# Two more quads of edges bucketed in the last round of a graph-convolution kernel

## Chip, core and metric

The kernel runs on one core of a Trainium2 chip. The metric is the device time of one execution in microseconds (us). The program is one launch; all times below are of that one core.

## What is computed

A pre-normalised graph convolution over 6250 nodes with 128 features and 200000 edges. Cut to what matters:

```python
h = maximum(layernorm(x), 0)
xw = h @ W_in                                       # per node
W_ij = (softplus(f_ij @ W_f1 + b_f1) - log 2) @ W_f2 + b_f2
m = xw[idx_j] * (W_ij * cutoff)                     # per edge; idx_j = dst
out = segment_sum(m, idx_i, num_segments=6250)      # idx_i = src
result = x + (softplus(out @ W_o1 + b_o1) - log 2) @ W_o2 + b_o2
```

`dst` is sorted, `src` is random. So the gather by `dst` reads narrow windows of a table, while the sum by `src` has to spread every edge's row over all nodes.

## The kernel before

**Tiling.** The edges are padded to 200704 (704 filler edges, with weight 0 and `src` 0) and worked in 391 *quads* of 512 edges, four chunks of 128 each. The main loop (its body is written out by the program) has one iteration i per quad, and a software pipeline runs through it: iteration i does the first matmul and the softplus of quad i, the gather matmuls and the second matmul of quad i-1 (`s2_pe_x`, `s2_pe_w`, L336 to L347), the scaling on ScalarE (L352), and the product m on VectorE (L357).

**Two ways to sum by node.** A *plain* quad is summed within each chunk by a matmul with an equality matrix (`s1_eq` L318, `s3_pe` L369), copied out of PSUM (`s3_copy` L377, five buffers `s`), given its row numbers (`s3_idx` L391, `s3_ji` L398), and added to an accumulator in DRAM by GpSimd: `scatter`, L417, one indirect DMA with add for each chunk. Four accumulators take turns (`acc_of`); one of them, accumulator 0, takes no scatter from number `RET` on, the total less 64, so that it can be read back into the SBUF accumulator `accT` during the last iterations (`r0_load` L866, `r0_tp` L873, `r0_add` L880).

A *bucketed* quad sends nothing by itself. Its 512 edges are ranked into 16 buckets of 392 nodes with 32 slots each, with 64 overflow slots for what finds no room (`rank_group` to `rank_slot`, one call for each eight quads). `perm_oh` (L503) builds a permutation matrix, `part_rem` (L517, L520) splits the messages into three bf16 parts, `permute` (L527, four matmul groups s = 0 to 3) sorts them into the slots, and `perm_out` (L533) copies each group to a tile `mst`. The overflow of two bucketed quads together goes through a short chain (`over_pe` L542 to L544, `over_out`, `over_idx`, `over_dg`, `over_row` L571, `over_eq` L576, `over_sum` L581, `over_copy`, `over_ji`, `over_int`) to a single scatter.

**Rounds and units.** Eight bucketed quads make a round. A round's slots are added up in SBUF by four *units*, one for each s: `unit_oh` (L605) builds a one-hot tile for each quad on VectorE, `unit_pe` (L620) runs 12 matmuls for each quad into four PSUM banks of tag B, all four of them, and `unit_evac` (L631) adds the four banks to `accT`. A unit's matmuls are in iteration k, its `unit_oh` in k-1, its `unit_evac` in k+1.

**Which quads, and where.** `sorted_quads` starts at quad 8 and steps by 2 and 3 in turn while q < 391 - `MPEND`, then cuts the list to full rounds: with `MPEND` 4 it is 8, 10, 13, ... 383, 385, that is 152 quads, 19 rounds. `unit_slots` puts the units of a round into iterations of the next round; those of the last round come at its last quad + 6, + 8, + 10, + 12: 391, 393, 395, 397. All of this is an order written out by hand: the hooks `at(i, point, ...)` fix each engine's program order, and each engine works in that order.

**After the loop** a flag is computed from the largest overflow (`dmax`, L994, to `flagi`, L1004). If a quad's overflow has exceeded its 64 slots, a loop over all 1563 chunks (L1007) does the sum again in a slow way; otherwise the loop runs no trip. Then the tail loads accumulators 1 to 3 (`t_load`, L1075), adds them (L1081, L1087), adds `accT` (L1098) and applies the output layers.

Of the kernel before, what the change touches and what calls it, by code (L numbers as in the profile page):

```python
# [7 lines left out]
F32 = mybir.dt.float32  # L8
BF16 = mybir.dt.bfloat16
# [11 lines left out]
P = 128  # L21
# [5 lines left out]
SLOTS = GRP * CAP + OVC  # L27
MP0 = 8
MPGAPS = (2, 3)
MPEND = 4  # L30
RND = 8
RKQ = 8
PW = 387
MW = 388
# [12 lines left out]
def tile_gnn(ctx: ExitStack, tc: tile.TileContext, x, fB, cT, srcT, srcr, dstr, win_, wf1, wf2, bias, bo1c, wo1,  # L47
# [20 lines left out]
    GN = NP // GRP  # L68
# [4 lines left out]
    mpq = sorted_quads(NQ)  # L73
# [12 lines left out]
    cp = ctx.enter_context(tc.tile_pool(name="cp", bufs=1))  # L86
# [3 lines left out]
    wk = edge.enter_context(tc.tile_pool(name="wk", bufs=2))  # L90
# [19 lines left out]
    win_sb = cp.tile([P, P], F32, name="win_sb")  # L110
    w1f = wk.tile([K1, P], F32, tag="a", name="w1f")
    w2 = cp.tile([P, P], F32, name="w2")
    bf = cp.tile([P, P], F32, name="bf")
    bo2b = cp.tile([P, P], F32, name="bo2b")
    bo1_sb = cp.tile([P, 1], F32, name="bo1_sb")
    nbo1 = cp.tile([P, 1], F32, name="nbo1")
# [10 lines left out]
    thr = cp.tile([P, GRP - 1], F32, name="thr")  # L127
    ge = cp.tile([P, 4 * RKQ, GRP + 1], BF16, name="ge")
    dropT = cp.tile([P, EP // P], BF16, name="dropT")
# [44 lines left out]
    def prep_norm(g):  # L174
        o, T = groups[g]
        rs = wk.tile([P, 4], F32, tag="rs", name="rs", bufs=1)
        r0 = pst[g]["r0"]
        nc.vector.tensor_tensor(rs[:, :T], r0[:, :T], r0[:, :T], op=ALU.mult)
        nc.vector.tensor_tensor(rs[:, :T], rs[:, :T], pst[g]["var"][:, :T], op=ALU.mult)
        nc.vector.tensor_scalar(rs[:, :T], rs[:, :T], -0.5, 1.5, op0=ALU.mult, op1=ALU.add)  # L180
        nc.vector.tensor_tensor(rs[:, :T], rs[:, :T], r0[:, :T], op=ALU.mult)
        xn = wk.tile([P, 4, P], F32, tag="rm", name="xn", bufs=1)
        for t in range(T):
            nc.vector.tensor_scalar(xn[:, t], x_sb[:, o // P + t], pst[g]["mv"][:, t, 0:1], rs[:, t:t + 1],
                                    op0=ALU.subtract, op1=ALU.mult)
        pst[g]["xn"] = xn
# [7 lines left out]

    def prep_relu(g):
        T = groups[g][1]
        h = wk.tile([P, 4, P], F32, tag="h", name="h", bufs=1)
        nc.scalar.activation(h[:, :T], pst[g]["hps"][:, :T], AF.Relu)
        pst[g]["h"] = h

# [6 lines left out]

    def prep_x1(g):
        T = groups[g][1]
        x3 = wk.tile([P, 4, 3, P], BF16, tag="x3", name="x3", bufs=1)  # L210
        nc.scalar.copy(x3[:, :T, 0], pst[g]["xs"][:, :T])
        pst[g]["x3"] = x3

    def prep_rm(g):
        T = groups[g][1]
        rm = wk.tile([P, 4, P], F32, tag="rm", name="rm", bufs=1)
        nc.vector.tensor_tensor(rm[:, :T], pst[g]["xs"][:, :T], pst[g]["x3"][:, :T, 0], op=ALU.subtract)
        pst[g]["rm"] = rm

# [201 lines left out]
    mp = {}  # L421
# [5 lines left out]
    def rank_group(r):  # L427
        qs = mpq[RKQ * r:RKQ * r + RKQ]
        nc4 = 4 * len(qs)
        srcf = wk.tile([P, 4 * RKQ], F32, tag="srcf", name="srcf", bufs=1)  # L430
        for k, q, d, n in runs(qs):
# [5 lines left out]
                                thr.unsqueeze(1).to_broadcast(n), op=ALU.is_ge)  # L437
        G = wk.tile([P, 4 * RKQ, GRP], BF16, tag="G", name="G", bufs=1)
        nc.vector.tensor_tensor(G[:, :nc4], ge[:, :nc4, :GRP], ge[:, :nc4, 1:], op=ALU.subtract)
        cnt = wk.tile([P, 4 * RKQ], F32, tag="cnt", name="cnt", bufs=1)  # L440
        nc.vector.tensor_reduce(cnt[:, :nc4], ge[:, :nc4, 1:GRP], axis=AX.X, op=ALU.add)
        loc = wk.tile([P, 4 * RKQ], F32, tag="loc", name="loc", bufs=1)
        nc.vector.scalar_tensor_tensor(loc[:, :nc4], cnt[:, :nc4], float(-GN), srcf, op0=ALU.mult, op1=ALU.add)
# [85 lines left out]
        mp[q]["q", s] = t  # L529

    def perm_out(q, s):
        mp[q]["ms", s] = wk.tile([P, MW], BF16, tag=f"ms{s}", name="mst", bufs=RND + 2 * s)
        nc.scalar.copy(mp[q]["ms", s][:, :PW], mp[q].pop(("q", s))[:, :PW])  # L533

    def over_pe(q):
# [63 lines left out]
        scatter(mp[q]["os"][:, :P], mp[q]["ji"][:, 0:1])  # L599

    def unit_oh(r, s):
        for q in mpq[r * RND:(r + 1) * RND]:
            so = wk.tile([P, GN], BF16, tag="so", name="so", bufs=RND)
            w = mp[q]["ms", s].bitcast(F32)
            nc.vector.tensor_scalar(so, iotw[:, :GN], w[:, 3 * P // 2:3 * P // 2 + 1], None, op0=ALU.is_equal)  # L605
            mp[q]["oh"] = so
# [3 lines left out]
    def unit_pe(r, s):  # L610
        ts = []
        for g in range(4):
            t = ps.tile([P, 512], F32, tag="B", name="un", bufs=4)
            ts.append(t)
        qs = mpq[r * RND:(r + 1) * RND]
        for q in qs:
            for k in range(3):
                for g in range(4):
                    v = slice(g * CAP, (g + 1) * CAP)
                    nc.tensor.matmul(ts[g][:, :GN], mp[q]["ms", s][v, k * P:(k + 1) * P], mp[q]["oh"][v],  # L620
                                     start=(q == qs[0] and k == 0), stop=(q == qs[-1] and k == 2))
        un[r, s] = ts
# [47 lines left out]
    with tc.manual_schedule():  # L670
# [91 lines left out]
        ms = []  # L762
# [88 lines left out]

        def late_bias():
            nc.vector.tensor_scalar(nbo1, bo1_sb, -1.0, None, op0=ALU.mult)
            bb = wk.tile([P, 4, P], F32, tag="rm", name="bb", bufs=1)
            nc.vector.tensor_copy(bb[:, 0], bo1_sb.to_broadcast([P, P]))
            bps = ps.tile([P, 4, P], F32, tag="B", name="bps", bufs=4)
            nc.tensor.matmul(bps[:, 0], bb[:, 0], wo2_sb, start=True, stop=True)
            late["bps"] = bps
# [74 lines left out]
        last = mpq[-1]  # L933
        for r in range(len(mpq) // RND):
            for s, k in enumerate(unit_slots(mpq, r)):
# [71 lines left out]
    with tc.For_i(0, trips, 1) as ci:  # L1007
# [17 lines left out]
        x3 = wk.tile([P, 3, P], BF16, tag="pt", name="fx3")  # L1025
# [29 lines left out]
        s = wk.tile([P, P], F32, bufs=1, tag="dg", name="fs")  # L1055
# [112 lines left out]
def sorted_quads(nq):  # L1168
    qs, q = [], MP0
    while q < nq - MPEND:  # L1170
        qs.append(q)
        q += MPGAPS[(len(qs) - 1) % len(MPGAPS)]
    return qs[:len(qs) // RND * RND]


def unit_slots(qs, r):
    nxt = [qs[n] + 2 for n in range(RND * (r + 1), min(RND * (r + 2), len(qs))) if qs[n] - qs[n - 1] == 3]
    return nxt[:4] if nxt else [qs[-1] + 6 + 2 * s for s in range(4)]


# [49 lines left out]
def _layout(inputs):  # L1230
    import numpy as np

    p = "L0_gnn_"
    x = np.asarray(inputs["x"])
    src, dst = np.asarray(inputs["src"]), np.asarray(inputs["dst"])
    f, c = np.asarray(inputs["edge_attr_20"]), np.asarray(inputs["edge_weight1"])
    n, e = x.shape[0], src.shape[0]
    rb = f.shape[1]
    be = 4 * SC
    np_ = -(-n // P) * P  # L1240
    ep = -(-e // be) * be
    pad = ep - e
    xp = np.pad(x, ((0, np_ - n), (0, 0)))
    fp = np.pad(f, ((0, pad), (0, 0)))
    srcp = np.pad(src, (0, pad))
    dstp = np.pad(dst, (0, pad), mode="edge")
    n_sc = ep // SC
    caps = np.array(base_caps(np_, n_sc), np.float32)
    lane = np.arange(P)
    con = np.zeros((P, 16), np.float32)  # L1250
    con[:, 0] = lane % HB // 3
    con[:, 1] = np.power(3.0, 63.0 - lane)
    con[:, 2] = 2.0 * con[:, 1]
    con[:, 3] = np_ + lane
    con[:, 4] = 0.5
    con[:, 13] = lane
    con[:, 14] = np_ // GRP // 2 - con[:, 3]
    con[:n_sc // 2, 5] = caps[:n_sc // 2]
    con[:n_sc // 2, 6] = caps[n_sc // 2:]
    part = np.array([0, 1, 2, 0, 1, 0])  # L1260
    for r in range(6 * rb + 3):
        con[r, 7 + (part[r // rb] if r < 6 * rb else r - 6 * rb)] = 1.0
    for r in range(3):
        con[r, 10 + r] = con[HB + r, 10 + r] = 1.0
    idt = np.eye(P).astype(np.float32)
    wf1, bf1 = np.asarray(inputs[p + "W_f1"]), np.asarray(inputs[p + "b_f1"])
    return {
        "x": xp,
        "fB": fp.reshape(-1, be, rb).transpose(0, 2, 1),
        "cT": np.pad(c[:, 0], (0, pad)).reshape(-1, P).T,  # L1270
        "srcT": srcp.reshape(-1, P).T,
        "srcr": srcp.reshape(-1, SC),
        "dstr": dstp.reshape(-1, SC),
        "win": np.asarray(inputs[p + "W_in"]),
        "wf1": np.concatenate([wf1] * 6 + [bf1[None]] * 3, 0),
        "wf2": np.asarray(inputs[p + "W_f2"]),
        "bias": np.stack([np.asarray(inputs[p + "b_f2"]), np.asarray(inputs[p + "b_o2"])]),
        "bo1": np.asarray(inputs[p + "b_o1"]).reshape(-1, 1),
        "wo1": np.asarray(inputs[p + "W_o1"]),
        "wo2": np.asarray(inputs[p + "W_o2"]),  # L1280
        "consts": con,
        "ident": idt,
    }
# [19 lines left out]
```

## Time and profile before

| | |
|---|---|
| median of 3 runs | 2121.98 us (2119.21 to 2124.13) |
| the profiled execution | 2119.3 us, its span 2117.0 us |
| busy: TensorE, VectorE, ScalarE, GpSimd | 90%, 83%, 85%, 80% of the span |
| indirect scatters | 955 of plain chunks + 76 of overflow pairs |
| last matmul of quad 390's second layer | about 2006.4 us |
| last unit's matmuls end | 2047.2 us |
| last scatter's GpSimd instruction | 2058.57 to 2060.11 us |
| first load of the tail | 2062.44 us |

Views used are: the page with the busy shares and the costliest groups of instructions ("line engine operation, output<-input, count | busy us, mean ns of one | idle us just before, and what ended it"); the list of waits ("who <- for whom: us, times, longest"); the chain that ended last in order of time; the timeline ("start us, length us, engine, line, operation, count [idle before <- what ended it]"); and busy time by windows. PE is TensorE, DVE VectorE, ACT ScalarE, POOL GpSimd, SP SyncE; a "q" behind an engine is its instruction queue.

### The profile page before, as it was taken

The page shows a single profiled execution, that of the slowest core. Times are in us where ns is not written, and L with a number is a line of the kernel's source. Part 1 is how long each engine was busy: PE and PEld are TensorE (multiplying, and loading weights), DVE is VectorE, ACT ScalarE, POOL GpSimd, SP SyncE. Part 2 cuts the span into 40 slices and gives each one's busy share as a digit, 9 for nine tenths or more (in the row PEclk, how much of TensorE's full clock was granted, in tenths as well). Part 3 has the DMA queues.
Part 4 walks back from the last instruction along what each step waited for, and adds up shares of the span by engine and source line. Part 5 has one row for each costly group of instructions (what it writes and reads, how often), then busy time and mean ns, then how long its engine had stood idle before and what let it go on. Part 6 is the DMA issues. An engine that isn't in the chain of part 4 may idle for free.

```text
span 2117.0 us, 56533 instructions
## 1 busy us (share of the span) xinstructions
PE 1915.6 (90%) x19769; PEld 1392.3 (66%) x19769; DVE 1763.7 (83%) x4710; ACT 1789.3 (85%) x4781; POOL 1695.6 (80%) x1073
## 2 busy tenths in 40 slices
PE   3778999999999999998989999999999999998946
PEld 2556667676666667666767677777767666766724
DVE  4768888888989898888898989889888878897825
ACT  4688889998988899898989999999899898988804
POOL 2678888888888888888888888888888888887874
PEclk9899999999999999999999999999999999999977
DMA  7987767777777777777777777777777777777639
GB/s 265 242 183 132 149 129 146 141 157 144 149 141 147 133 151 145 141 145 142 148 133 157 139 136 152 143 146 152 136 146 139 129 152 137 139 154 144 111 38 241
DMA packets 395696, 315.17 MB, mean 149 GB/s; under 512 B 94959, under 2 KB 335130, under 8 KB 395410
## 3 DMA queue, kind: packets, MB, share of 16 engines
q1 hardware_dynamic: 245858, 240.57, 38.9%
q0 software_dynamic: 149264, 70.91, 35.3%
q8 instruction: 155, 2.54, 0.5%
q14 instruction: 131, 1.07, 0.2%
q10 hardware_dynamic: 288, 0.07, 0.0%
HBM read 173.32 MB, written 138.06 MB: 147 GB/s over the span
## 4 chain that ended last, share of the span: by engine, by line
PE 32%; ACT 20%; DVE 19%; DMA 10%; POOL 10%; issue 7%; SPq 2%; ACTq 0%; DVEq 0%; POOLq 0%
POOL acc L417 10%; DMA acc<-s,ji 8%; PE un L620 8%; PE W L347 7%; PE pq L527 6%; ACT xc L352 5%; PE pp L369 4%; ACT mst L533 3%; DVE so L605 3%; ACT e L295 3%; ACT e L294 2%; ACT e L300 2%; DVE pm L503 2%; ACT s L377 2%; DVE a L324 1%
## 5 line engine op out<-in xcount | busy, mean ns | idle before, releaser
L417 POOL DMA_INDIRECT acc<-s,ji x955 | 1538.3, 1611 | 350.3 <-issue 222.8
L527 PE MATMUL pq<-pt,pm 128*128 128x387 bf16 x2432 | 484.1, 339 | 26.5 <-ACT s L377 19.2
L352 ACT ACTIVATE xc<-xg,cb 128x128 f32<-128x128 f32 x1564 | 446.4, 374 | 46.9 <-PE xg L339 45.0
L347 PE MATMUL W<-w,a 128*128 128x128 f32 x3128 | 461.7, 292 | 0.0
L347 PEld LDWEIGHTS W<-w,a 128*128 128x128 f32 x3128 | 386.2, 194 | 41.8 <-issue 2.3
L620 PE MATMUL un<-so,mst 32*128 32x392 bf16 x7296 | 355.1, 331 | 41.8 <-DVE pr L467 18.4
L527 PEld LDWEIGHTS <-pm 128*128 128x128 bf16 x2432 | 238.6, 99 | 187.7 <-issue 36.1
L620 PEld LDWEIGHTS <-mst 32*128 32x128 bf16 x7296 | 223.0, 94 | 169.3 <-issue 63.0
L324 DVE SCALAR_TENSOR_TENSOR a<-z,e 128x512 f32<-128x512 f32 x391 | 267.2, 683 | 70.2 <-ACT e L300 70.0
L300 ACT ACTIVATE e<-e,con 128x512 f32<-128x512 f32 x391 | 282.3, 722 | 12.7
L369 PEld LDWEIGHTS pp<-m,eq 128*128 128x128 f32 x1912 | 255.0, 195 | 37.2 <-DVE accT L631 23.6
L369 PE MATMUL pp<-m,eq 128*128 128x129 f32 x1912 | 261.4, 280 | 17.0 <-DVE accT L631 15.0
L533 ACT CAST mst<-pq 128x387 bf16<-128x387 f32 x608 | 260.4, 480 | 8.3 <-PE pq L527 8.3
L377 ACT COPY s<-pp 128x258 f32<-128x258 f32 x478 | 167.1, 391 | 116.2 <-PE pp L369 64.8
L295 ACT ACTIVATE e<-e 128x512 f32<-128x512 f32 x391 | 246.5, 630 | 12.4
L294 ACT ACTIVATE e<-z 128x512 f32<-128x512 f32 x391 | 242.0, 619 | 16.7 <-PE z L289 16.1
L357 DVE TENSOR_TENSOR m<-W,xc 128x512 f32<-128x512 f32 x239 | 164.0, 686 | 80.4 <-ACT xc L352 75.4
L517 DVE TENSOR_TENSOR pt<-pt 128x512 f32<-128x512 f32 x304 | 209.9, 691 | 0.0
L503 DVE TENSOR_SCALAR pm<-iot,pos 128x576 bf16<-128x576 f16 x608 | 197.5, 387 | 0.0
L631 DVE TENSOR_TENSOR accT<-un,accT 128x392 f32<-128x392 f32 x288 | 142.5, 556 | 47.3 <-PE un L620 32.1
L357 DVE TENSOR_TENSOR pt<-W,xc 128x512 f32<-128x512 f32 x152 | 104.5, 688 | 82.1 <-ACT xc L352 80.7
L289 PE MATMUL z<-ft,ws 123*128 123x512 bf16 x391 | 151.9, 389 | 17.9 <-DMA ft<-fsd 17.9
(156 smaller groups left out, 2693.2 us busy)
## 6 DMA issues: line engine op xcount, KB each, us to landing
sb<-src SPq DMA_DIRECT2D x195, 256.0 KB
ft<-fsd SPq DMA_DIRECT2D x195, 240.0 KB
rb<-reld SPq DMA_DIRECT2D x391, 64.0 KB
fsd<-f SPq DMA_DIRECT2D x49, 480.0 KB
fb<-in_fB_dram SPq DMA_DIRECT2D x49, 320.0 KB
fsd<-f SPq DMA_DIRECT2D x49, 320.0 KB
acc<-s,ji POOLq DMA_INDIRECT x955
wn<-tab SPq DMA_DIRECT2D x782, 15.8 KB
```

The source lines that it names most:

```text
L294: nc.scalar.activation(e, st[q]["z"], AF.Abs)
L295: nc.scalar.activation(e, e, AF.Exp, scale=-1.0)
L300: nc.scalar.activation(e, e, AF.Ln, bias=half, scale=0.5)
L324: nc.vector.scalar_tensor_tensor(a, st[q]["z"], 0.0, st[q]["l"], op0=ALU.max, op1=ALU.add)
L347: nc.tensor.matmul(W[:, c, :], st[q]["a"][:, c * P:(c + 1) * P], w2, start=False, stop=(c == 3))
L352: nc.scalar.mul(xc[:, c, :], st[q]["xg"][:, c, :], late["c", q // CQ][:, 4 * (q % CQ) + c:4 * (q % CQ) + c + 1])
L357: nc.vector.tensor_tensor(m[:, :, :P], st[q]["W"], st[q]["xc"], op=ALU.mult)
L369: nc.tensor.matmul(pp[:, c, :129], st[q]["eq"][:, k, :], m[:, k, :129], start=True, stop=True)
L417: nc.gpsimd.indirect_dma_start(out=accs[k][:, :], out_offset=bass.IndirectOffsetOnAxis(ap=ji, axis=0), in_=s, in_offset=None, compute_op=A ...
L527: nc.tensor.matmul(t[:, :PW], mp[q]["pm"][:, c, s * P:(s + 1) * P], high(mp[q]["pt"][:, c:c + 1, :PW])[:, 0], start=(c == 0), stop=(c == 3))
L533: nc.scalar.copy(mp[q]["ms", s][:, :PW], mp[q].pop(("q", s))[:, :PW])
L620: nc.tensor.matmul(ts[g][:, :GN], mp[q]["ms", s][v, k * P:(k + 1) * P], mp[q]["oh"][v], start=(q == qs[0] and k == 0), stop=(q == qs[-1] a ...
```

## The change

The bound of `sorted_quads` becomes the last quad, so that the list goes on with 388 and 390: 154 quads. They are two over 19 full rounds; up to two (`EXTRA`) such quads are kept, and the last round takes all of them, so it has ten quads. Its units move with the last quad to iterations 396, 398, 400, 402. A 20th ranking group, of two quads, comes in iterations 383 to 387. To hold ten quads, `so` and two of the `mst` tags have ten buffers in place of eight; the room comes from tiles whose width of four groups was never filled beyond two (`xn`, `h`, `x3`, `rm`), from `bb`, and from `bf`, which moves into the buffer of tag `dg`. The fillers' sources become 0, 48, 96, ... modulo 6250 in place of 0.

```diff
-MPEND = 4
+MPEND = 0
 RND = 8
+EXTRA = 2
...
-    bf = cp.tile([P, P], F32, name="bf")
+    bf = wk.tile([P, P], F32, tag="dg", name="bf", bufs=1)
...
-        xn = wk.tile([P, 4, P], F32, tag="rm", name="xn", bufs=1)
+        xn = wk.tile([P, 2, P], F32, tag="rm", name="xn", bufs=1)
...
-        mp[q]["ms", s] = wk.tile([P, MW], BF16, tag=f"ms{s}", name="mst", bufs=RND + 2 * s)
+        mp[q]["ms", s] = wk.tile([P, MW], BF16, tag=f"ms{s}", name="mst", bufs=RND + max(EXTRA, 2 * s))
...
     def unit_oh(r, s):
-        for q in mpq[r * RND:(r + 1) * RND]:
-            so = wk.tile([P, GN], BF16, tag="so", name="so", bufs=RND)
+        for q in round_quads(mpq, r):
+            so = wk.tile([P, GN], BF16, tag="so", name="so", bufs=RND + EXTRA)
...
-        qs = mpq[r * RND:(r + 1) * RND]
+        qs = round_quads(mpq, r)
...
-    return qs[:len(qs) // RND * RND]
+    return qs if len(qs) % RND <= EXTRA else qs[:len(qs) // RND * RND]
+
+
+def round_quads(qs, r):
+    last = len(qs) // RND - 1
+    return qs[r * RND:] if r == last else qs[r * RND:(r + 1) * RND]
 
 
 def unit_slots(qs, r):
-    nxt = [qs[n] + 2 for n in range(RND * (r + 1), min(RND * (r + 2), len(qs))) if qs[n] - qs[n - 1] == 3]
+    last = len(qs) // RND - 1
+    nxt = [qs[n] + 2 for n in range(RND * (r + 1), min(RND * (r + 2), len(qs) if r < last else 0)) if qs[n] - qs[n - 1] == 3]
...
-    srcp = np.pad(src, (0, pad))
+    srcp = np.concatenate([src, (np.arange(pad) * (n // P) % n).astype(src.dtype)])
```

More of the change, by code (lines that the diff above doesn't have):

```diff
@@ L196, in prep_relu @@
         T = groups[g][1]
-        h = wk.tile([P, 4, P], F32, tag="h", name="h", bufs=1)
+        h = wk.tile([P, 2, P], F32, tag="h", name="h", bufs=1)
         nc.scalar.activation(h[:, :T], pst[g]["hps"][:, :T], AF.Relu)
@@ L209, in prep_x1 @@
         T = groups[g][1]
-        x3 = wk.tile([P, 4, 3, P], BF16, tag="x3", name="x3", bufs=1)
+        x3 = wk.tile([P, 2, 3, P], BF16, tag="x3", name="x3", bufs=1)
         nc.scalar.copy(x3[:, :T, 0], pst[g]["xs"][:, :T])
@@ L215, in prep_rm @@
         T = groups[g][1]
-        rm = wk.tile([P, 4, P], F32, tag="rm", name="rm", bufs=1)
+        rm = wk.tile([P, 2, P], F32, tag="rm", name="rm", bufs=1)
         nc.vector.tensor_tensor(rm[:, :T], pst[g]["xs"][:, :T], pst[g]["x3"][:, :T, 0], op=ALU.subtract)
@@ L853, in late_bias @@
             nc.vector.tensor_scalar(nbo1, bo1_sb, -1.0, None, op0=ALU.mult)
-            bb = wk.tile([P, 4, P], F32, tag="rm", name="bb", bufs=1)
+            bb = wk.tile([P, 1, P], F32, tag="rm", name="bb", bufs=1)
             nc.vector.tensor_copy(bb[:, 0], bo1_sb.to_broadcast([P, P]))
```

## The prediction, made before the change was run

> **What bounds the kernel now.** I read the page first: four engines are over 80% busy, so the shares decide nothing. Then GpSimd's rows:
>
> ```profile
> L417 POOL DMA_INDIRECT acc<-s,ji x955 | 1538.3, 1611 | 350.3 <-issue 222.8
> ...
> POOL acc L417 <- issue: 230.4, 748, 2.4
> POOL acc L417 <- DMA acc<-s,ji: 50.9, 81, 5.4
> ```
>
> The 955 plain scatters take 1.54 us each in the usual case, with 0.30 us of issue behind each: most of GpSimd's "idle" time is that fixed gap. A scatter so costs 1.845 us of GpSimd's time, and the 955 + 76 of them some 1900 of the 2060 us before the tail. GpSimd is the bound, with a backlog. The timeline of the end shows how far behind it is:
>
> ```profile
> 2045.64 1.54 POOL L417 DMA_INDIRECT acc<-s,ji  x1 [0.31 <-issue]
> ...
> 2047.23 1.04 DVE L631 TENSOR_TENSOR accT<-un,accT 128x392 f32<-128x392 f32 x2 [4.22 <-PE un L620]
> ...
> 2056.72 1.54 POOL L417 DMA_INDIRECT acc<-s,ji  x1 [0.30 <-issue]
> 2058.57 1.54 POOL L417 DMA_INDIRECT acc<-os,oji  x1 [0.31 <-issue]
> 2062.44 7.02 SPq L1075 DMA_DIRECT2D ta_in<-acc  x9
> 2062.76 1.04 DVE L631 TENSOR_TENSOR accT<-un,accT 128x392 f32<-128x392 f32 x2 [14.49 <-DMA acc<-os,oji]
> ```
>
> Quad 390's products are done near 2010, yet its three scatters are those from 2053.03 to 2056.72, and the overflow scatter of 383/385 at 2058.57 is last. Two things follow. The end of the edge phase is GpSimd's last scatter, its landing, and 0.65 us to the tail's first load. And there is a meeting of all engines there: the last two evacuations of the last unit wait 14.49 us although PE was done, and start with SP. What is ahead of them (the last unit's matmuls, its first two evacuations) must be done before the tail may start. The chain of waits agrees on the landing (3.22 us from 2058.57):
>
> ```profile
> 2058.57 3.22 DMA acc<-os,oji
> 2062.44 0.38 SPq L1075
> ```
>
> Last, the four units of the last round, each the same 96 matmuls, by windows (us, PE busy, DVE busy, granted clock, ...):
>
> ```profile
> 2016.00:2022.67 6.67, 6.67 (x95) 0.12 (x1) 0.63 0.46 42
> 2027.00:2032.82 5.82, 5.82 (x93) 0.12 (x1) 0.71 0.42 37
> 2034.97:2039.15 4.18, 4.18 (x96) 0.00 (x0) 1.00 0.46 43
> 2041.43:2047.21 5.78, 5.78 (x96) 0.00 (x0) 0.71 0.38 34
> ```
>
> At full clock a matmul costs 4.18 / 96 = 43.5 ns, at half clock 87; the four windows hold some 5.0, 3.3, 0 and 3.2 us at half clock.
>
> **GpSimd's side.** Removed: four scatters of quad 388 and three of quad 390; added: one overflow scatter for the pair. Six fewer: 6 x 1.845 = 11.07 us. GpSimd ends at 2060.11 - 11.07 = 2049.04, landed (3.22 - 1.54 = 1.68 later) at 2050.7, tail at 2051.4. This holds only if GpSimd stays fed. Its order becomes 386, 387, 389, overflow 383/385, overflow 388/390; quad 389's first scatter would come at 2038.1 and its rows are ready near 2012; the new overflow scatter would come at 2047.2 (below).
>
> **The other engines, iterations 383 to 395.** Each of the two quads loses, by the timeline near 2000: DVE eq 0.68 and jf 0.21, PE 1.05 (L369), ACT 0.82 + 0.30. It gains: DVE 1.4 (four L503) and 0.69 + 0.20 + 0.69 (L517, L520); PE 4 x 0.70 (L527) and 0.75 (twelve L542 to L544); ACT 4 x 0.43 (L533) and 0.26. The pair's overflow chain adds under 1 us on each engine; ranking two quads adds some 15 short DVE operations (0.15 to 0.3 us: 3 to 4 us). dmax (1.78 us on DVE, at 1887.1 now) needs the last ranking and moves to iteration 387 or later, with a small DMA on SP. Taken away there: 2.08 us of DVE for the first unit's one-hots, now in iteration 395. DVE's net is +6 us through iteration 391. What covers it: ACT's copies of plain rows (L377) wait for GpSimd's landings anyway (3.08 us at 2008.04, 5.19 us at 2015.57 with 6.39 us on PE behind it). With 388 plain no more, 389's copy reuses the buffer of 381 and not of 382, landed near 2007.9. And accumulator 0 takes its last scatter some four places earlier in GpSimd's order; its first read-back, now issued at 1932.37 as a scatter to it ends, held PE for 3.62 us at 1935.27 and can go up to 7 us earlier. I take the additions as covered through quad 390's second layer, 2006.4 as now; uncovered they cost up to 3 us; if the read-back gain outlasts the back-pressure, up to 1 us is won.
>
> **The chain to the last unit** replaces a stretch now hidden under the backlog. After 2008.9 (quad 389's copy) PE has the permutes of 388 and 390, two overflow groups and one overflow sum: 2.8 + 0.75 + 0.25 + 2.8 + 0.75 = 7.35 us, to 2016.3; about 1 us for the four PSUM banks, each waiting for ACT's copy; 0.75 us for the last copy out, the overflow index and the first one-hot. The first unit starts at 2018.3 (I allow 2016 to 2021.5). It has 120 matmuls, 5.22 us at full clock. Full for the first (PE has just been busy); 3.3 us at half clock for the second and last as in the rows, +1.65 each: 5.22 + 6.87 + 5.22 + 6.87 = 24.2. Gaps by the windows: 4.33 (evacuation, one-hots, overflow row and its comparison), 2.15, 2.28, plus 0.5 for two more one-hots ahead of the comparison: 9.3. Last matmul 2018.3 + 33.5 = 2051.8; two evacuations 1.04; 0.65 to the tail: 2053.5. In this chain the overflow sum of 388/390 comes after the second unit, near 2036.5, its scatter is ready by 2041: in time. So the unit chain passes GpSimd by 2 us and sets the end: 2062.44 - 2053.5 = 9.0 us gained, of GpSimd's 11.07.
>
> **The skill against the rows.** "TensorE: Matmul & The Clock Gate" (Part 1) has the clock halve only after an idle window of about 3.4 us. By it, gaps of 2.2 us keep units three and four at full clock: 1.65 us off. But the row of the fourth shows 0.71 after 2.28 us; I take the row. "SBUF — State Buffer" (SBUF: two separate sides) speaks against the change: VectorE in a two-port mode locks GpSimd out of writing descriptors. The change adds eight L605 (0.26 us each) and eight L503 (0.35) while scatters run, 4.9 us; locked out for all that, GpSimd would save 6.2 us and not 11.1. The rows: eight L605 lie over a scatter that takes its usual 1.54 us, so I take none of it:
>
> ```profile
> 2024.58 2.11 DVE L605 TENSOR_SCALAR so<-iot,mst 128x392 bf16<-128x392 f16 x8
> ...
> 2025.09 1.54 POOL L417 DMA_INDIRECT acc<-s,ji  x1 [0.30 <-issue]
> ```
>
> **The rest costs nothing:** wider rings only loosen waits that the unit spacing of five iterations already leaves empty; the narrowed tiles keep their operations' shapes; the fillers' weight stays 0.
>
> **The tail** (2062.44 to the end, 54.6 us) is not touched. Sum against the profiled 2119.3 (span 2117.0, 2.3 around it): 2110.3. The median of the runs lies 2.7 above that execution: 2121.98 - 9.0 = 2113.0.
>
> **Rivals.** (a) As above, gain 6 to 11, 2111 to 2116: 0.62. (b) GpSimd alone sets the end, the unit chain being quick enough (first unit at 2016, full clock in three units): 11.1, and up to 13 with fewer stalls on read-backs: 2109 to 2111; for it GpSimd's unbroken 0.30 us gaps, against it 33 us of units: 0.10. (c) The additions are not covered, the units 5 us each at half clock (5.22 + 2.5 = 7.7; 31 in all): gain 9 - 6.7 = 2.3, with a late start about 0: 2115 to 2122: 0.21. (d) Slower: the drain never gets the full clock. Four units of 120 x 87 ns = 41.8 us put the end at 2018.3 + 41.8 + 9.3 + 1.7 = 2071.1, 8.7 us later than now: 2130.7. It decides once the units exceed 33.1 us together, 8.3 each; for it the two windows at 0.63 and 0.71, against it that longer bursts warm up, as all four did: 0.06. (e) The change doesn't do what it says: an overflow over 64 starts the loop over 1563 chunks, at over 3.7 us (two indirect DMAs) a trip, milliseconds. In the reference's inputs quad 390 has 320 edges and 192 fillers; with fillers at 0 one bucket would hold 207 and 175 would overflow, spread 34 do; quad 388 has 27: 0.01.
>
> **Numbers.** About 0.2%, 4.2 us, is what a measurement of this kernel can tell from no change. Faster by more: (a), (b) and a good third of (c) less some scatter of the runs: 0.80; within: 0.13; slower: 0.07. The range, 2109.0 to 2119.5, takes in (b) and most of (c).
>
> **What would show it.** Right: GpSimd's last scatter an overflow near 2047 with 0.30 us gaps before it; ten-quad units with 120 matmuls; the last unit's matmuls ending at 2050 to 2054, the tail's first load 1.7 us behind. Wrong: a first unit later than 2022, units over 7.5 us each, GpSimd waiting for ACT's row numbers, or a difference in any window before 1925.

## The result, and the profile after

| | before | after |
|---|---|---|
| median, 8 runs each | 2122.32 us (2118.21 to 2127.37) | 2107.97 us (2103.64 to 2115.75) |
| ratio | | 0.9943, 95% interval 0.9928 to 0.9959 |
| the profiled execution, its span | 2119.3, 2117.0 us | 2109.0, 2107.2 us |
| last unit's matmuls end | 2047.2 us | 2051.1 us |
| last scatter's instruction ends | 2060.1 us | 2048.7 us |
| first load of the tail | 2062.44 us | 2052.52 us |
| tail | 54.6 us | 54.7 us |

The change is faster by 12.1 us by the ratio (8.7 to 15.3), by 9.9 at the tail's first load of the two profiles. The tail takes the same time in both, so the gain lies ahead of it. The timeline of the changed kernel's end (start, length, engine, line, operation, count, idle before):

```profile
2043.68 1.98 DVE L632 TENSOR_TENSOR accT<-un,accT 128x392 f32<-128x392 f32 x4 [2.80 <-PE un L621]
2045.19 1.54 POOL L418 DMA_INDIRECT acc<-os,oji  x1 [0.30 <-DMA acc<-s,ji]
2045.59 2.87 DVE L606 TENSOR_SCALAR so<-iot,mst 128x392 bf16<-128x392 f16 x10
2045.95 5.16 PE L621 MATMUL un<-so,mst 32*128 32x392 bf16 x120 [2.28 <-DVE so L606]
...
2047.04 1.63 POOL L418 DMA_INDIRECT acc<-os,oji  x1 [0.30 <-DVE so L606]
2051.12 1.04 DVE L632 TENSOR_TENSOR accT<-un,accT 128x392 f32<-128x392 f32 x2 [2.66 <-PE un L621]
2052.52 4.16 SPq L1076 DMA_DIRECT2D ta_in<-acc  x7
2053.88 1.04 DVE L632 TENSOR_TENSOR accT<-un,accT 128x392 f32<-128x392 f32 x2 [1.72 <-issue]
```

GpSimd is done with its last scatter at 2048.67, six scatters sooner, and the tail does not start then. It starts 0.36 us after the second evacuation of the last unit, which has ten quads (x120, x10). Before, the last two evacuations stood 14.49 us behind GpSimd's landing; now what is ahead of the meeting is the unit itself. The page's row of the scatters holds seven fewer, and the overflow group one more:

```profile
L418 POOL DMA_INDIRECT acc<-s,ji x948 | 1523.7, 1607 | 348.1 <-issue 225.6
```

**How to read the runs below.** Executions reach the last quads at times that differ by some microseconds, whatever the kernel: quad 390's last W matmul ends at 2006.4 in the kernel before and at 2010.6 in e1, which has the same order of work up to there. So I read two distances in each profile: from the end of the last scatter's instruction to the tail's first load, and from the last unit's last matmul to the same. The one that stands at its smallest value names the chain that set the end.

| kernel | ratio to before (95%) | last scatter to tail, us | last unit to tail, us | set by |
|---|---|---|---|---|
| before | | 2.33 | 15.23 | GpSimd |
| after | 0.9943 (0.9928 to 0.9959) | 3.85 | 1.41 | units |
| e0, after again | 0.9961 (0.9941 to 0.9980) | 4.73 | 1.41 | units |
| e1 | 0.9999 (0.9988 to 1.0011) | 2.32 | 14.54 | GpSimd |
| e2 | 0.9961 (0.9947 to 0.9976) | 2.44 | 6.48 | GpSimd |
| e3 | 0.9978 (0.9963 to 0.9993) | 2.59 | 6.96 | GpSimd |
| e5 | 0.9964 (0.9952 to 0.9977) | 7.13 | 1.41 | units |
| e7 | 0.9941 (0.9921 to 0.9961) | 11.26 | 1.40 | units |
| e8 | 0.9938 (0.9916 to 0.9961) | 2.49 | 2.40 | GpSimd, by little |
| e9 | 0.9930 (0.9912 to 0.9949) | 8.77 | 1.29 | units |

To see where a gain arises, I also measure from two scatters, numbered from 0 as `RET` numbers them. Number 900, near 1806 us, is well ahead of everything that the change moves at the end; the profiles reach it between 1800.9 and 1810.8 us, so that much of a difference in absolute times can be there before the change does anything. Number 1015 is close to the last place up to which the order of the scatters is the same in all kernels (number 1018). All times in us:

| kernel | scatter 900 to 1015 | 1015 to the tail's first load | 900 to quad 390's last W matmul |
|---|---|---|---|
| before | 224.4 | 31.8 | 200.2 |
| e1 | 224.0 | 31.7 | 199.8 |
| e2 | 223.8 | 20.8 | 199.5 |
| after | 220.9 | 22.2 | 198.8 |
| e0 | 223.2 | 23.2 | 201.1 |
| e7 | 222.8 | 23.2 | 200.8 |
| e8 | 223.1 | 20.9 | 200.9 |
| e9 | 221.8 | 19.8 | 199.6 |
| e3 | 221.2 | 26.3 | 199.1 |
| e5 | 224.8 | 25.5 | 204.4 |

### The profile page after: what moved, and what is told of

It is laid out like the page before. It is cut to its first block, busy times and chain, and to the rows that moved or that the text cites. A ratio compares the mean times of both kernels' runs of the same rounds, so it can differ in the third digit from the quotient of the medians.

```text
span 2107.2 us, 56868 instructions
## 1 busy us (share of the span) xinstructions
PE 1926.4 (91%) x19917; PEld 1402.2 (67%) x19917; DVE 1774.3 (84%) x4749; ACT 1793.4 (85%) x4789; POOL 1685.2 (80%) x1067
## 5 line engine op out<-in xcount | busy, mean ns | idle before, releaser
L621 PE MATMUL un<-so,mst 32*128 32x392 bf16 x7392 | 359.4, 329 | 35.1 <-DVE pr L468 14.8
L295 ACT ACTIVATE e<-z 128x512 f32<-128x512 f32 x391 | 241.7, 618 | 18.5 <-PE z L290 17.8
L504 DVE TENSOR_SCALAR pm<-iot,pos 128x576 bf16<-128x576 f16 x616 | 202.0, 389 | 0.0
```

Of the source, the lines that this page charges most:

```text
L295: nc.scalar.activation(e, st[q]["z"], AF.Abs)
```

## The experiments

The theory: the gain is the six scatters that GpSimd no longer has, 11.07 us, cut down where the later and longer chain of the last round's units ends after GpSimd. The rivals: the buffers or moved tiles, the earlier read-back of accumulator 0, GpSimd alone.

**e1: everything but the two quads.**

```diff
-MPEND = 0
+MPEND = 4
```

> The changed kernel with MPEND back at 4: 152 bucketed quads as before, but all the new buffers, narrowed tiles and spread filler sources. My theory (the gain is six scatters less on GpSimd, minus what the later unit chain takes back): no difference from before, 0 us, ratio 1.000, the tail's first load at 2062 to 2063 us. Rival, that the wider rings or the moved tiles give the gain: 5 to 10 us faster, ratio 0.995 to 0.998.

Measured: ratio 0.9999, nothing within 2.5 us either way. Rings, narrowed tiles and spread fillers give nothing by themselves. (First load at 2066.5 and not 2062: this execution came 4.2 us later to quad 390.)

**e2: six scatters off the kernel before.** The rows of quad 388 and of two of quad 390's three chunks are left out of the sums.

```diff
-        for c in range(nchunks(q)):
+        for c in range({388: 0, 390: 1}.get(q, nchunks(q))):
```

> The kernel before, with six scatters left out (the four of quad 388 and two of the three of quad 390), nothing else changed; those rows are missing from its sums. My theory: GpSimd ends 6 x 1.845 = 11.07 us earlier and nothing is late behind it, since the units of the last round end near 2047 us as before: the tail's first load at 2051.4, 11.1 us faster, 1.2 us more than the changed kernel's 9.9 by the profiles. Rival, that GpSimd's backlog is not what sets the end: under 4 us.

Measured: 8.3 us faster (5.1 to 11.2), so the 11.1 lies at the upper edge of the interval and the rival's 4 outside it. The profile says it more closely: from quad 390's W matmul to the end of the last scatter it is 42.64 us, 53.69 before: 11.05 less for six scatters.

```profile
2047.51 1.04 DVE L631 TENSOR_TENSOR accT<-un,accT 128x392 f32<-128x392 f32 x2 [2.67 <-PE un L620]
2047.94 1.54 POOL L417 DMA_INDIRECT acc<-s,ji  x1 [0.31 <-issue]
2049.79 1.54 POOL L417 DMA_INDIRECT acc<-os,oji  x1 [0.30 <-issue]
2053.77 2.79 SPq L1075 DMA_DIRECT2D ta_in<-acc  x5
```

GpSimd still ends last, with the last unit's matmuls 4.0 us ahead of it: the relief alone is not used up.

**e3: one quad, not two.**

```diff
-MPEND = 0
+MPEND = 2
```

> The changed kernel with MPEND 2: only quad 388 is bucketed in addition, nine quads in the last round, 390 plain. Four scatters go, one overflow scatter of 388 alone comes: three fewer, 5.5 us. The units are in iterations 394 to 400, two earlier than with 390, so they end before GpSimd does. My theory: GpSimd sets the end, first load of the tail at 2056.9, 5.5 us faster than before. Rival, that the units set the end here too: first load near 2051, 9 to 11 us faster. Rival, buffers: 10 us faster as with both quads.

Measured: 4.7 us faster (1.5 to 7.8) against 5.5 expected and 9 to 11 of the rivals. With half the scatters saved half the gain comes, and GpSimd sets the end (2.59 us), the last unit's matmuls being 4.4 us ahead. The first load stands at 2048.8 and not at 2056.9: this execution was 4.9 us early at scatter 900 and gained another 3.3 us up to scatter 1015. From there to the tail it takes 5.5 us less than before, as expected.

**e5: accumulator 0 given up at the old scatter number.**

```diff
-    RET = max(120, sum(scat) - 64)
+    RET = max(120, sum(scat) - 58)
```

> The changed kernel, with accumulator 0 given up six scatters later, at the number at which the kernel before gives it up (967 of 1025). My theory: the first read-back again waits about 7 us longer and may hold TensorE for up to 3.6 us near 1935, but the copies of plain rows, which wait for GpSimd's landings, take most of that up: 0 to 2 us slower than the changed kernel, 8 to 10 us faster than before. Rival, that the freed read-back wait is a part of the gain: 3 to 4 us slower than the changed kernel.

Measured: 7.6 us faster than before (4.9 to 10.2); the changed kernel had 12.1 and 8.3, so run times can't tell the two kernels apart. The profile shows two waits again that the changed kernel's profiles don't have, one of TensorE (3.62 us in the kernel before) and one of GpSimd:

```profile
1933.66 1.09 PE L874 MATMUL rtp<-idt,r0t 128*128 128x128 f32 x4 [3.36 <-DMA r0t<-acc]
...
1935.53 1.54 POOL L418 DMA_INDIRECT acc<-s,ji  x1 [2.44 <-DMA acc<-s,ji]
```

The second neither the prediction nor the expectation had. It stands in the kernel before too:

```profile
1937.02 1.54 POOL L417 DMA_INDIRECT acc<-s,ji  x1 [2.54 <-DMA acc<-s,ji]
```

This is scatter number 967, the first that takes its turn among three accumulators. By `acc_of`, number 966 goes to accumulator 2 (966 modulo 4), and number 967 to accumulator 2 again (1 + 967 modulo 3), so it waits for the landing just ahead of it: 2.44 to 2.54 us in the four profiles with this `RET` (before, e1, e2, e5). With `RET` 961 the last scatter to the same accumulator is three back, and the first of the new turn is preceded by 0.30 to 1.04 us in the six profiles of it. That six fewer scatters put the hand-over on a better turn is luck, not design.

With both waits back, the table has quad 390's W matmul 4.2 us later than in the kernel before, and from scatter 900 the tail's first load comes 3.9 us later than in e0 and 7.2 later than in the changed kernel's first profile. So the rival is not excluded: the earlier retirement of accumulator 0, six scatters sooner, is a part of the gain, and may well be worth 3 to 4 us. This one profile can't divide it between the two waits.

**e0 and e7: the changed kernel again, and without quad 389's four scatters** (its rows are left out of the sums).

```diff
-        for c in range(nchunks(q)):
+        for c in range(0 if q == 389 else nchunks(q)):
```

> The changed kernel once more, on the chip and between the same runs as the three below, so that they can be read against it: 8.7 to 15 us faster than before by its first eight runs, by its profile 9.9 us; the tail's first load near 2052.5 us.

> The changed kernel with the four scatters of quad 389, the last plain quad, left out (its rows are missing from the sums). GpSimd then ends 7.4 us earlier, near 2043 landed. My theory (the chain of the last round's units sets the end of the edge phase): no gain over the changed kernel, 0 to 0.5 us, last unit's matmuls at 2051 and the first load of the tail at 2052 as with them. Rival, that GpSimd still sets the end: 7.4 us faster than the changed kernel.

Measured: e0 8.3 us faster than before (4.2 to 12.5). e7 12.5 (8.3 to 16.7): the intervals overlap, and the times alone can't exclude either theory. The profiles do. GpSimd ends 6.6 us sooner against quad 390's W matmul (34.05 us after it, 40.63 in e0), and the tail's first load stands where it stood (45.31, 45.36):

```profile
2040.96 1.54 POOL L418 DMA_INDIRECT acc<-os,oji  x1 [1.48 <-ACT oji L596]
...
2045.52 6.84 PE L621 MATMUL un<-so,mst 32*128 32x392 bf16 x120 [2.28 <-DVE so L606]
2052.36 1.04 DVE L632 TENSOR_TENSOR accT<-un,accT 128x392 f32<-128x392 f32 x2 [4.82 <-PE un L621]
2053.76 4.63 SPq L1076 DMA_DIRECT2D ta_in<-acc  x7
```

GpSimd even waits 1.48 us for the overflow rows here, and is idle from 2042.50 on. Nothing comes of it: the units set the end.

**e8: one-hots ahead of the evacuations, in the last round.** With the ring of ten buffers each one-hot of the next unit is made as the unit before frees its buffer.

```diff
-            mp[q]["oh"] = so
+            mp[q]["oh", s] = so
...
-                at(k - 1, "D2", unit_oh, r, s)
+                at(k - (2 if r == len(mpq) // RND - 1 and s else 1), "D2", unit_oh, r, s)
```

> The changed kernel with the one-hots of the last round's second, third and fourth unit one iteration earlier, so that VectorE makes each as the unit before frees its buffer, ahead of that unit's four evacuations. The gaps between units shrink from 4.9, 2.2 and 2.3 us to some 2.9, 1.0 and 1.0: the last unit's matmuls end 4 us earlier, near 2047. My theory: GpSimd's last landing, near 2050.3, takes over as the end: first load at 2051, 1.5 us faster than the changed kernel and not 4. Rival, that the units alone count: 4 us faster. Rival, that the end is GpSimd's already: 0.

Measured: 13.1 us faster than before (8.3 to 17.8); 4.9 more than e0, 1.0 more than the changed kernel's first runs, in intervals too wide for either. In the profile the units end 40.62 us after quad 390's W matmul (42.85 and 43.95 with the changed kernel), and the tail starts at 43.02 (44.26, 45.36): 1.2 to 2.3 us sooner, where I gave 1.5.

```profile
2037.34 5.13 PE L621 MATMUL un<-so,mst 32*128 32x392 bf16 x117 [0.15 <-DVE accT L632]
...
2040.84 1.54 POOL L418 DMA_INDIRECT acc<-os,oji  x1 [0.31 <-issue]
2042.36 1.04 DVE L632 TENSOR_TENSOR accT<-un,accT 128x392 f32<-128x392 f32 x2 [5.07 <-PE un L621]
2044.87 3.39 SPq L1076 DMA_DIRECT2D ta_in<-acc  x6
```

The last unit is 1.0 us ahead of what the tail would need of it (2.40 where the units set the end at 1.4), and the tail follows GpSimd's last scatter by 2.49 us, as where GpSimd sets the end: the two chains end almost together. It has the lowest median of the kernels that compute everything, 2103.57 us, though not shown faster than the change by the runs.

**e9: e8 without quad 389's scatters** (rows left out as in e7).

> Both of the two edits above: one-hots ahead, and quad 389's four scatters left out. My theory (the later of the two chains sets the end): now neither holds at 2050, the units end near 2047, first load near 2048.5, 4 us faster than the changed kernel, although the first edit alone gives 0 and the second 1.5. Rival, GpSimd alone: 7.4; rival, the units alone: 4 here and 4 with the one-hots alone.

Measured: 14.8 us faster than before (10.8 to 18.6). The tail starts 41.90 us after quad 390's W matmul, 2.4 to 3.5 sooner than the changed kernel (4 expected; the gaps between units shrank less, below). Taking GpSimd's four scatters away gives nothing with the units late (e7), and 1.1 us once they are early (e8 to e9). The later of the two chains sets the end.

**e6: the filler sources at 0 again.**

```diff
-    srcp = np.concatenate([src, (np.arange(pad) * (n // P) % n).astype(src.dtype)])
+    srcp = np.pad(src, (0, pad))
```

> The changed kernel with the filler edges' sources at 0 again. Quad 390 then has 207 of its 512 edges in the first bucket, 175 in all over, for 64 overflow slots: the flag is set and the loop over 1563 chunks runs. My theory: several milliseconds to tens of milliseconds longer (over 3.7 us for two indirect DMAs in each trip, 5.8 ms at the least), the edge phase ahead of it as with the changed kernel. Rival, that the spread of the fillers has no part in it: as the changed kernel.

Measured: 28071.7 us, in one run. The first indirect DMA of the loop over chunks, a gather that the other kernels never run, starts at 2045.57, ahead of the last unit's end:

```profile
2045.57 1.03 POOL L1027 DMA_INDIRECT fx<-tab,dcol  x1 [0.30 <-issue]
```

The loop takes 28071.7 - 2109 = 25963 us, 16.6 us for each of 1563 trips. So the spread of the fillers brings no time, but without it the last quad may not be bucketed.

## Why the prediction was right, step by step

The direction and the chain that ends last were as forecast: GpSimd's relief, cut short by the units. The median of 2107.97 us is 5.0 under the 2113.0 and 1.0 under the range's lower end; by the ratio, taken off the median before, it is 2110.2. The gain of 9.0 us lies in the intervals of both comparisons (8.7 to 15.3, and 4.2 to 12.5 in e0), so the run times don't show its size wrong.

The profiles show that the sum is right for what it added up, and leaves something out. From scatter 1015 to the tail the changed kernel takes 9.6 us less than before, 8.6 in e0 and in e7. Ahead of that the sum has nothing, but for "up to 1 us". But from scatter 900 to 1015 the six profiles that have the changed kernel's order up to there (e6 is the sixth) take 220.9 to 223.2 us, those of before, e1 and e2 223.8 to 224.4: 1.6 us between the means. With accumulator 0 retired at the old number (e5: 224.8) that is gone.

- **GpSimd's side: right in the six scatters, short of a wait.** e2 gives 11.05 us for the six by themselves. The last scatter was expected from 2047.2 to 2049.04 and found from 2047.04 to 2048.67, fed without a gap; that it agrees so well is in part luck, since this execution was 3.3 us late at scatter 900 and made that up by scatter 1015.
- **"I take the additions as covered through quad 390's second layer, 2006.4 as now": right, but only with the earlier retirement.** The matmul ended at 2008.26, in an execution that was 3.3 us late at scatter 900. From there it comes 198.8 to 201.1 us later in the changed order, 199.5 to 200.2 in that of before. With the late retirement (e5) it is 204.4: uncovered, the additions cost 4 us there, where I gave up to 3.
- **First unit at 2018.3: found at 2018.87, by luck.** From quad 390's W matmul it is 10.5 to 10.6 us in each profile of two added quads, where I had 11.9: the PSUM banks were handed over without the 1 us I gave them (TensorE worked from 2010.21 to 2018.03 without a wait), and my terms add up to 2018.0, not 2018.3. The late execution hid this.
- **Units: 33.5 us expected, 32.2 found** (2018.87 to 2051.11), and 33.3 in e0. The bursts were not the ones I named:

```profile
2018.87:2024.02 5.15, 5.15 (x120) 0.00 (x0) 1.00 0.46 41
2028.89:2036.36 7.47, 7.46 (x117) 0.11 (x1) 0.68 0.40 38
2038.52:2043.68 5.16, 5.15 (x120) 0.00 (x0) 1.00 0.36 32
2045.95:2051.11 5.16, 5.16 (x120) 0.00 (x0) 1.00 0.34 32
```

  The second unit was longer at half clock than the 3.3 us I took (7.47 us at a granted clock of 0.68 are 4.8 us of it), the fourth not at all. In e0 the fourth was:

```profile
2045.61:2052.45 6.84, 6.83 (x120) 0.00 (x0) 0.75 0.33 31
```

- **Clock gate, skill against row: neither holds alone.** After a gap of 2.27 to 2.36 us the fourth unit had the full clock in the changed kernel and in e2 (4.16 us for 96), and half clock for a part in the kernel before, e1 (5.84 for 96), e0, e5, e6 and e7 (6.84 in the last four). The 3.4 us of "TensorE: Matmul & The Clock Gate" (Part 1) is not a safe gap here. The same section says that the window runs free of the work, and these traces agree: the granted clock is 1.00 or 0.50 and steps only at multiples of 3.41 us, which lie differently in each execution. In the six, at least 2.19 us of the gap fall between two such instants, and the clock is 0.50 from the second one on; in the changed kernel an instant cuts the gap into 0.23 and 2.04 us, in e2 into 1.25 and 1.03. TensorE's busy time and the granted clock (the column behind the count) from instant to instant, first in e0, then in the changed kernel:

```profile
2042.71:2046.12 3.41, 1.05 (x29) 1.00 0.35 28
2046.12:2049.53 3.41, 3.41 (x50) 0.50 0.35 35
...
2043.91:2047.32 3.41, 1.37 (x36) 1.00 0.36 34
2047.32:2050.74 3.42, 3.42 (x88) 1.00 0.45 43
```

  No safe length follows: 2.03 us of idle time between two instants, ahead of the changed kernel's second unit, did bring half clock. I should have given the fourth unit both values, 1.65 us apart.
- **Port lock: right to take none of it.** Ten one-hots from 2045.59 to 2048.46 lie over a scatter of 1.63 us, 0.09 over the usual. In the whole profile, 99 scatters that lie under one-hots (L606) for 0.8 us or more take 1.60 us on average, all of them 1.61.
- **Rivals.** (b), GpSimd alone, falls by e7, though its "fewer stalls on read-backs" did come and the ratio's 2110.2 us lies in its range and not in (a)'s. (c) and (d), the additions uncovered or the clock low throughout, did not come: three of four units had the full clock throughout, two in e0. (e) is what e6 shows, with the fillers at 0: milliseconds.
- **Size.** The second comparison (e0) gives 8.3 us, the first 12.1. From scatter 900 to the tail's first load the two profiles give 9.8 and 13.2 us, 1.1 of the 3.4 between them by the units. I can't say from these runs where in 8 to 12 us the gain lies, nor, beyond e5, how much of it belongs to the retirement.

## What to carry to other kernels

When the engine with the backlog is relieved, look at what the other engines had finished unseen under that backlog, and lay that chain out with its own gaps and clock: here 33 us of units took back 1.5 to 2.5 of 11 us. An edit that changes a count also moves everything numbered by it: six fewer scatters moved the retirement of an accumulator, and a wait of 2.5 us went with it. Where all engines meet, the distance from the last instruction of each to the first behind the meeting names the one that sets the end, in a profile whose absolute times wander by more than the effect. And a filler value is a part of the data's distribution: 192 equal indices were harmless in a sum and would fill a bucket.

## What was not expected of the hardware

- A burst of 120 matmuls took 5.16 or 6.84 us after the same 2.3 us of idle time, by where the clock's window fell; 2.0 us of it in one window of 3.41 us could be enough for half clock.
- A scatter to the accumulator of the scatter just ahead of it waited 2.4 to 2.5 us for the landing, four times in four profiles.
- In e8 the gaps between units shrank less than expected: before each burst proper the first matmuls into the four banks wait for one evacuation each, 0.47 us apart (2035.92, 2036.39, 2036.86, 2037.34 ahead of the fourth unit).
- A trip of the loop over chunks takes 16.6 us, though its two indirect DMAs take 1.01 and 1.58 us of GpSimd: in the list of groups GpSimd's idle time before the gather is put down to the small loads of columns ahead of it, and as much again, before the scatter, to no wait that the profile shows.
